# Pairwise outer products with batch normalisation: the statistics regrouped, with TensorE sums, one shift per input and another load order

## The chip, the cores and the metric

The kernel runs on one core of a Trainium2 chip. A core has five engines that run their own instruction streams side by side: TensorE (PE, matrix products), VectorE (DVE), ScalarE (ACT), GpSimd (POOL) and SyncE (SP, which here only starts DMA transfers). They meet by semaphores. Inputs and output lie in HBM; the engines work on SBUF (128 partitions), and TensorE writes to PSUM. The metric is the device time of one execution in microseconds (us). The kernel before takes 1874.52 us, the median of 7 runs (1874.37 to 1874.97).

## What is computed

The reference, cut to what matters:

```python
B, F0, F1, E, C = (256, 39, 39, 16, 1)          # the inputs themselves hold 1024 samples
_ROWS, _COLS = np.tril_indices(F1, k=-1)         # the 741 pairs row > col
cross  = xj[:, rows, :, None] * xi[:, cols, None, :]
mean   = jnp.mean(cross, axis=(0, 2, 3), keepdims=True)
var    = jnp.mean(jnp.square(cross - mean), axis=(0, 2, 3), keepdims=True)
normed = (cross - mean) * jax.lax.rsqrt(var + BN_EPS)
normed = normed * gamma[None, :, None, None] + beta[None, :, None, None]
out    = normed[:, :, None, :, :] * W[None, None, :, :, :]
```

xi and xj are 1024 x 39 x 16 in f32. For each sample and each of 741 pairs of fields a 16 x 16 outer product is formed, normalised with one mean and one variance per pair (over all samples and all 256 elements), scaled by gamma and beta of the pair and multiplied element by element by the 16 x 16 matrix W. The output is 1024 x 741 x 256 f32, 777 MB; the inputs are 6 MB.

## The kernel before

**Layout.** Sample 8p + t lies in partition p at place t, so a partition holds eight samples (NT = 8). xi_sb and xj_sb hold the inputs whole. The output is made in tiles: one row r of the triangle (r pairs) for two places t (T = 2). y_sb has room for four tiles of the middle row (r = 19) at first; the scratch tiles of the statistics lie in the parts of y_sb that later tiles take (`scratch`, parts "dev" and "rest").

**Statistics.** The mean of an outer product over its 256 elements is the product of two sums, and the mean square the product of two sums of squares. So the statistics of all pairs come from three Gram matrices over the samples, of 38 rows and 77 columns (`gram`, three accumulators ps_g; the right-hand side fb has for each place t 38 means of xi, 38 second moments and a constant). To keep precision, the data are shifted first: `sums` adds up the 16 elements of each field (VectorE), a matrix of ones on TensorE sums those of place 0 over all partitions, and this gives one shift per field and input. `deviation` subtracts the shift (GpSimd, eight steps of two places), `square` squares in place (ScalarE), `moments` adds up 16 squares (VectorE), `means` corrects the sums by the shift, `gram` multiplies. The `steps` tuple gives the order of the eight steps.

**From the Gram matrices to the scale.** A chain of small 38 x 38 steps on ScalarE, GpSimd and VectorE forms mean and variance of each pair, the reciprocal (VectorE), a square root (ScalarE, rstd) and one refinement step (VectorE) to stq, which holds scale and offset. `spread` sends row r of stq to all partitions by a matmul with the selecting matrix pick (row r of it has ones where the partition is r - 1; GpSimd makes it by one affine_select), and `apply` joins it with gamma and beta in st_sb. This goes by row groups, the group of row 19 first.

**The first tiles.** So that stores can start as soon as the scale is known, the raw outer products of tile 0 are made before: 32 products of 304 elements, one for each (t, i), by `raw_products`: steps 0 to 23 on ScalarE (raw0), 24 to 31 on GpSimd (raw0_pool), given out in small lots by `emit` between other work. After the scale is known, `affine` applies scale and offset to tile 0 in place (pairs 0 and 1 on VectorE, the others in turn on ScalarE and GpSimd), `weigh` multiplies by W on VectorE in six pieces and stores each. From tile 1 on, `scale_xi` scales xi (GpSimd), `products` makes outer products (ScalarE, and some on GpSimd), `finish` adds the offset and multiplies by W (VectorE, a few pairs on GpSimd) and stores.

**Order.** The whole is under a manual schedule: every engine executes its instructions in the order in which the code emits them, and waits at the head of its queue. DMA starts are instructions of the queue of the engine that starts them (SP and ACT here). There are eight semaphores for DMAs, so each DMA start also waits for the landing of the one eight before it.

Of the kernel before, what the change touches and what calls it, by code (L numbers as in the profile page):

```python
# [9 lines left out]
ALU = mybir.AluOpType  # L10
# [4 lines left out]
T = 2  # L15
# [11 lines left out]

LOADS = (1, 2, 3, 4, 6, 8)
# [15 lines left out]
def tile_pair_outer_batchnorm(  # L44
# [58 lines left out]
    place = {"dev": half * EE, "rest": (half + half // 2) * EE}  # L103
    stop = {"dev": (half + half // 2) * EE, "rest": 2 * half * EE}
# [18 lines left out]
    devs = [scratch("dev", P, T, G, E) for _ in range(7)]  # L123
    ones = scratch("rest", P, P)
    pick = scratch("rest", G, G, P)
    total = scratch("rest", P, NT, 2 * G)
    fa = scratch("rest", P, NT, 2 * G)
    fb = scratch("rest", P, NT, 2 * G + 1)
    shift = scratch("rest", P, 2, G)
    shift_r = scratch("rest", G, 1)  # L130
    g1 = scratch("rest", G, 2 * G + 1)
    u_u, u_2 = (scratch("rest", G, 1) for _ in range(2))
    k, q1, q2, q3, uv, uv_2, v_half, mixed, low, mean, rstd, inv = (scratch("rest", G, G) for _ in range(12))
# [13 lines left out]
    def product(n, engine, t, i, src):  # L147

        r, t0, _ = tiles[n]
        y = view(n).rearrange("p t n (i j) -> p t n i j", j=E)[:, t, :, i, :]  # L150
        scale = xj_sb[:, t0 + t, r, i : i + 1]
        if engine is nc.scalar:
            nc.scalar.activation(y, src, AF.Copy, scale=scale)  # L153
        else:
            engine.tensor_scalar(y, src, scale, 1.0, ALU.mult, ALU.mult)  # L155
# [167 lines left out]
    with tc.manual_schedule():  # L323
        nc.gpsimd.memset(ones, 1.0)
        nc.sync.dma_start(xi_sb[:, 0, 0 : F // 2], xi_v[:, 0, 0 : F // 2])
        nc.scalar.dma_start(xi_sb[:, 0, F // 2 : F], xi_v[:, 0, F // 2 : F])
        nc.sync.dma_start(xj_sb[:, 0], xj_v[:, 0])
        def load(engine, to, source, t0, t1):
            engine.dma_start(to[:, t0:t1], source[:, t0:t1])

        for t0, t1 in zip(LOADS, LOADS[1:-2]):
            load(nc.sync, xj_sb, xj_v, t0, t1)
            load(nc.scalar, xi_sb, xi_v, t0, t1)


        nc.scalar.activation(shift_r, ones[0:G, 0:1], AF.Sqrt)
        load(nc.sync, xj_sb, xj_v, *LOADS[-3:-1])
        nc.gpsimd.memset(fb[:, :, 2 * G : 2 * G + 1], 1.0 / NB)

        nc.gpsimd.affine_select(  # L340
            out=pick, in_=ones[0:G, :].unsqueeze(1).to_broadcast([G, G, P]),
            compare_op=ALU.is_equal, fill=0.0, base=0,
            pattern=[[-1, G], [0, P]], channel_multiplier=1,
        )
# [5 lines left out]
        k_s = 1.0 / (P * E)  # L350
        sources = (xj_sb[:, :, 1:F], xi_sb[:, :, 0:G])

        def part(x):
            return slice(x * G, (x + 1) * G)

        def sums(t0, t1, xs=(1, 0)):
            for x in xs:
                nc.vector.tensor_reduce(  # L358
                    total[:, t0:t1, part(x)], sources[x][:, t0:t1], AX.X, ALU.add
                )  # L360

        steps = ((0, 1), (0, 0), (2, 1), (4, 1), (6, 1), (2, 0), (4, 0), (6, 0))

        def deviation(n):
            t0, x = steps[n]
            nc.gpsimd.tensor_tensor(  # L368
                devs[n % 7],
                sources[x][:, t0 : t0 + T],  # L370
                shift[:, x : x + 1, :].unsqueeze(3).to_broadcast([P, T, G, E]),
                ALU.subtract,
            )

        def square(n):

            _, x = steps[n]
            scale = 0.25 / NB**0.5 if x else 0.25
            nc.scalar.activation(devs[n % 7], devs[n % 7], AF.Square, scale=scale)  # L379

        def moments(n, t0, t1):
            first_t, x = steps[n]
            to = fb if x else fa
            nc.vector.tensor_reduce(  # L384
                to[:, t0:t1, G : 2 * G], devs[n % 7][:, t0 - first_t : t1 - first_t], AX.X, ALU.add
            )

        def means(t0, t1):
            for x, to in enumerate((fa, fb)):
                stt(  # L390
                    to[:, t0:t1, 0:G],
                    total[:, t0:t1, part(x)],
                    1.0 / (E * NB) if x else 1.0 / E,
                    ps_u[:, x : x + 1, :].to_broadcast([P, t1 - t0, G]),
                    ALU.mult,
                    ALU.subtract,
                )

        def gram(n, t0, t1):
            x = steps[n][1]  # L400
            for t in range(t0, t1):
                terms = ((0, fa[:, t, 0:G]), (2, ones[:, 0:G])) if x else ((1, fa[:, t, G : 2 * G]),)
                for acc, lhs in terms:
                    nc.tensor.matmul(  # L404
                        ps_g[acc][0:G, 0 : 2 * G + 1], lhs, fb[:, t], start=t == 0, stop=t == NT - 1
                    )

        raw0 = raw_products(0, nc.scalar, range(24))
        raw0_pool = raw_products(0, nc.gpsimd, range(24, 32))
        ps_shift = (ps_g[0][:, 0:G], ps_s[:, 0:G])  # L410
        for x in (1, 0):
            sums(0, 1, (x,))
            nc.tensor.matmul(ps_shift[x], ones, total[:, 0, part(x)], start=True, stop=True)
        nc.tensor.matmul(ps_c[0:G, 0:1], total[:, 0, 0:G], ones[:, 0:1], start=True, stop=True)

# [179 lines left out]
```

## Time and profile before

The profiled execution took 1874.54 us; its span from the first to the last instruction is 1872.8 us.

| view | figure | value |
|---|---|---|
| times | median of 7 runs | 1874.52 us |
| profiled execution | time / span | 1874.54 / 1872.8 us |
| busy share of the span | DVE / ACT / POOL / PE | 92% / 85% / 83% / 1% |
| DMA | bytes, mean rate | 783.61 MB, 418 GB/s |
| chain that ended last | DMA of the output | 57% |
| timeline | first store issued | 34.10 us |
| GpSimd's deviations (L368) | 8 instructions of 1216 elements | 2265 ns mean |
| ScalarE's squares (L379) | 8 of 1216 elements | 1211 ns mean |
| VectorE's sums of 1216 elements (L358, L384) | | 1412 ns mean |
| raw products of 304 elements (L153 / L155) | ScalarE / GpSimd | 538 / 518 ns mean |
| Gram matmuls (L404) | 48 records, 77 columns | 337 ns mean |

The engines' shares are means over the whole span. A line such as "L153" is a line of the kernel and may be a helper that serves many stages, so the stage before the first store is read from stretches of the timeline. Instructions on an engine overlap a little: the mean duration of one is longer than the distance from one start to the next.

### The profile page before, as it was taken

What the parts mean: (1) busy time and instruction counts of PE and PEld (TensorE: products, weight loads), DVE (VectorE), ACT (ScalarE), POOL (GpSimd) and SP (SyncE); (2) the same over time, 40 slices, a digit from 0 to 9 for tenths busy, and PEclk for the clock granted to TensorE, in tenths of its full rate; (3) what the DMA queues carried; (4) which work ended last, traced back from release to release, by engine and by line L of the source; (5) the groups of instructions that cost most, each with busy time, mean ns of one, the idle gap of its engine ahead of it and who ended that gap; (6) DMA issues with size and microseconds to landing.
All of it is one profiled execution on the core that took longest, in us unless ns stands there. A gap on an engine that the chain in (4) does not pass through costs nothing.

```text
span 1872.8 us, 9236 instructions
## 1 busy us (share of the span) xinstructions
PE 26.0 (1%) x130; PEld 23.2 (1%) x130; DVE 1723.1 (92%) x2641; ACT 1584.4 (85%) x3152; POOL 1554.2 (83%) x1650
## 2 busy tenths in 40 slices
PE   5000000000000000000000000000000000000000
PEld 4000000000000000000000000000000000000000
DVE  8999888899999999999999999999999999999994
ACT  8999888898888867666799999999899998989892
POOL 9999877787777788999988888888888888888882
DMA  5999999999999999999999999999999999999998
GB/s 214 390 419 424 426 430 422 425 426 427 425 427 425 427 426 424 429 425 421 417 435 425 426 432 426 425 431 426 426 431 426 430 426 430 427 429 425 429 427 355
DMA packets 54711, 783.61 MB, mean 418 GB/s; under 512 B 4720, under 2 KB 6384, under 8 KB 17520
## 3 DMA queue, kind: packets, MB, share of 16 engines
q1 hardware_dynamic: 53344, 779.72, 98.2%
q10 hardware_dynamic: 1296, 3.29, 0.5%
q14 instruction: 70, 0.57, 0.1%
q8 instruction: 1, 0.02, 0.0%
HBM read 6.00 MB, written 776.99 MB: 418 GB/s over the span
## 4 chain that ended last, share of the span: by engine, by line
DMA 57%; ACT 20%; DVE 16%; POOL 2%; issue 1%; SPq 0%; ACTq 0%; DVEq 0%; POOLq 0%
DMA out_dram<-y_sb 57%; ACT y_sb L153 20%; DVE y_sb L313 16%; POOL y_sb L155 1%; POOL y_sb L302 1%; ACT y_sb L250 0%; POOL y_sb L299 0%; POOL xs L175 0%; SPq L236 0%; ACT y_sb L297 0%; DVE y_sb L198 0%; DVE xs L188 0%; ACTq L153 0%; DVEq L590 0%; DVE st_sb L540 0%
## 5 line engine op out<-in xcount | busy, mean ns | idle before, releaser
L313 DVE SCALAR_TENSOR_TENSOR y_sb<-y_sb,st_sb,w_dve 128x512 f32<-128x512 f32 (+1 forms) x2511 | 1653.1, 739 | 114.5 <-issue 99.1
L153 ACT ACTIVATE y_sb<-xs,xj_sb 128x144 f32<-128x144 f32 (+23 forms) x2930 | 1453.3, 586 | 239.3 <-DMA out_dram<-y_sb 204.3
L302 POOL TENSOR_TENSOR y_sb<-y_sb,w_sb 128x2048 f32<-128x2048 f32 (+3 forms) x155 | 517.8, 3347 | 89.8 <-ACT y_sb L297 80.2
L155 POOL TENSOR_SCALAR y_sb<-xs,xj_sb 128x320 f32<-128x320 f32 (+19 forms) x1006 | 559.8, 581 | 9.1 <-DMA out_dram<-y_sb 8.8
L175 POOL TENSOR_TENSOR xs<-xi_sb,st_sb 128x640 f32<-128x640 f32 (+33 forms) x135 | 184.2, 1364 | 177.5 <-ACT y_sb L153 172.8
L299 POOL TENSOR_SCALAR y_sb<-y_sb,st_sb 128x512 f32<-128x512 f32 x291 | 197.6, 695 | 5.1 <-ACT y_sb L153 5.1
L297 ACT ACTIVATE y_sb<-y_sb,st_sb 128x512 f32<-128x512 f32 x160 | 100.2, 708 | 4.0 <-POOL y_sb L155 2.3
L208 POOL TENSOR_TENSOR y_sb<-xs,xj_sb 128x1280 f32<-128x1280 f32 (+2 forms) x24 | 66.7, 2799 | 0.0
L198 DVE TENSOR_TENSOR y_sb<-xs,ps 128x256 f32<-128x256 f32 (+3 forms) x32 | 24.8, 817 | 0.6
L522 PE MATMUL ps<-y_sb 38*128 38x38 f32 (+37 forms) x76 | 16.4, 397 | 2.9 <-DVE y_sb L508 2.9
L522 PEld LDWEIGHTS ps<-y_sb 38*128 38x128 f32 x76 | 16.3, 329 | 3.2 <-DVE y_sb L508 3.2
L379 ACT ACTIVATE y_sb<-y_sb 128x1216 f32<-128x1216 f32 x8 | 9.7, 1211 | 2.9 <-POOL y_sb L368 2.6
L153 ACT ACTIVATE y_sb<-xi_sb,xj_sb 128x304 f32<-128x304 f32 x24 | 11.4, 538 | 0.0
L384 DVE TENSOR_REDUCE y_sb<-y_sb 128x76 f32<-128x1216 f32 (+1 forms) x9 | 10.9, 1271 | 0.0
L259 DVE TENSOR_TENSOR y_sb<-y_sb,w_dve 128x2048 f32<-128x2048 f32 (+4 forms) x6 | 10.7, 1839 | 0.1
L368 POOL TENSOR_TENSOR y_sb<-xi_sb,y_sb 128x1216 f32<-128x1216 f32 x4 | 9.1, 2265 | 1.2 <-DMA xi_sb<-in_r_xi_dram 1.0
L358 DVE TENSOR_REDUCE y_sb<-xi_sb 128x38 f32<-128x608 f32 (+1 forms) x6 | 5.9, 990 | 3.8 <-DMA xi_sb<-in_r_xi_dram 3.8
L368 POOL TENSOR_TENSOR y_sb<-xj_sb,y_sb 128x1216 f32<-128x1216 f32 x4 | 9.0, 2266 | 0.0
L404 PE MATMUL ps<-y_sb 128*38 128x77 f32 x48 | 8.1, 337 | 13.3 <-DVE y_sb L384 13.2
L252 POOL TENSOR_SCALAR y_sb<-y_sb,st_sb 128x512 f32<-128x512 f32 x8 | 6.4, 815 | 1.9 <-ACT y_sb L153 1.9
L358 DVE TENSOR_REDUCE y_sb<-xj_sb 128x38 f32<-128x608 f32 (+1 forms) x6 | 6.0, 992 | 0.8 <-DMA xj_sb<-in_r_xj_dram 0.7
L250 ACT ACTIVATE y_sb<-y_sb,st_sb 128x512 f32<-128x512 f32 x9 | 6.5, 801 | 0.2 <-ACT y_sb L153 0.2
(60 smaller groups left out, 42.9 us busy)
## 6 DMA issues: line engine op xcount, KB each, us to landing
out_dram<-y_sb SPq DMA_DIRECT2D x16, 3072.0 KB, 21.7
out_dram<-y_sb SPq DMA_DIRECT2D x20, 2432.0 KB, 12.5
out_dram<-y_sb SPq DMA_DIRECT2D x10, 4608.0 KB, 15.1
out_dram<-y_sb SPq DMA_DIRECT2D x12, 3840.0 KB, 21.0
out_dram<-y_sb SPq DMA_DIRECT2D x16, 2816.0 KB, 22.3
out_dram<-y_sb SPq DMA_DIRECT2D x12, 3584.0 KB, 23.1
out_dram<-y_sb SPq DMA_DIRECT2D x12, 3328.0 KB, 24.3
out_dram<-y_sb SPq DMA_DIRECT2D x15, 2560.0 KB, 11.9
```

Source lines behind the costliest of these rows:

```text
L153: nc.scalar.activation(y, src, AF.Copy, scale=scale)
L155: engine.tensor_scalar(y, src, scale, 1.0, ALU.mult, ALU.mult)
L175: nc.gpsimd.tensor_tensor(xs, xi_sb[:, t0 : t0 + T, 0:r, :], s_sb[:, :, n0 : n0 + r, :].to_broadcast([P, T, r, E]), ALU.mult,)
L198: nc.vector.tensor_tensor(view(n)[:, t].rearrange("p n (i j) -> p n i j", j=E), xs[:, t].unsqueeze(2).to_broadcast([P, r, E, E]), xj_short ...
L208: nc.gpsimd.tensor_tensor(view(n)[:, t].rearrange("p n (i j) -> p n i j", j=E), xs[:, t].unsqueeze(2).to_broadcast([P, r, E, E]), xj_sb[:, ...
L297: nc.scalar.activation(y[:, :, c, :], y[:, :, c, :], AF.Identity, bias=t_c)
L299: nc.gpsimd.tensor_scalar(y[:, :, c, :], y[:, :, c, :], t_c, 1.0, ALU.add, ALU.mult)
L302: nc.gpsimd.tensor_tensor(y[:, :, c0:c1, :], y[:, :, c0:c1, :], w_sb.unsqueeze(1).to_broadcast([P, T, c1 - c0, EE]), ALU.mult,)
L313: stt(y[:, t : t + size, c, :], y[:, t : t + size, c, :], t_sb[:, n0 + c : n0 + c + 1], w_dve.to_broadcast([P, size, EE]), ALU.add, ALU.mult,)
L358: nc.vector.tensor_reduce(total[:, t0:t1, part(x)], sources[x][:, t0:t1], AX.X, ALU.add)
L368: nc.gpsimd.tensor_tensor(devs[n % 7], sources[x][:, t0 : t0 + T], shift[:, x : x + 1, :].unsqueeze(3).to_broadcast([P, T, G, E]), ALU.sub ...
L522: nc.tensor.matmul(ps[:, :, first[r] - n0 : first[r] - n0 + r], pick[:, r - 1, :], stq[:, :, 0:r], start=True, stop=True,)
```

## The change

The statistics are rewritten between the first load and stq; the tiles behind keep their code.

- One shift per input instead of one per field: `offset` multiplies the first 19 fields of place 0 by ones on TensorE (304 columns), and an activation with an accumulator sums the columns. The shift goes into the square's bias, so `deviation` and `means` are gone, and the correction of the sums moves into small 38 x 1 constants.
- The sums of the elements of four places of each input (xi: places 2 to 5, xj: 0 to 3) are made on TensorE: 16 matmuls with a unit matrix, one for each element, summed in PSUM (`matrix_sums`). The other places stay with VectorE (`sums`).
- Four of the squared blocks are halved by GpSimd (`fold`: element e plus element e + 8) before VectorE sums them.
- Loads: all of xi first, one place at a time, then xj, then gamma, beta and W. All but two are started by SP. Row 19 of xj for places 0 and 1 comes early, as a small load of its own (xj_first), and the raw products of tile 0 read it there.
- Raw products of tile 0: 20 on GpSimd (12 of them at the start), 12 on ScalarE (2 ahead of the square root, 10 behind it). The copy of W into PSUM (w_dve) follows them.
- pick is made in two parts: rows 18 to 38 at the start, rows 1 to 17 behind the affines of tile 0.

```diff
+        load(nc.scalar, xi_sb, xi_v, 2, 3)
+        nc.sync.dma_start(xj_first, xj_v[:, 0:T, mid])
+        load(nc.sync, xi_sb, xi_v, 1, 2)
+        for t in range(3, NT):
+            load(nc.sync, xi_sb, xi_v, t, t + 1)
+        for t0, t1 in ((0, 1), (1, 2), (2, 4), (4, 6), (6, 7), (7, 8)):
             load(nc.sync, xj_sb, xj_v, t0, t1)
-            load(nc.scalar, xi_sb, xi_v, t0, t1)
+        nc.sync.dma_start(st_sb[:, 0], gamma.partition_broadcast(P))
+        nc.sync.dma_start(st_sb[:, 1], beta.partition_broadcast(P))
+        nc.sync.dma_start(w_sb[:, 0, :], w.rearrange("o i j -> (o i j)").partition_broadcast(P))
...
+        picks(mid - 1, F)
...
+        def offset(x):
+            start = xi_sb[:, 0, 0:mid] if x else xj_sb[:, 0, 1 : mid + 1]
+            nc.tensor.matmul((ps_c, ps_s)[x][:, 0 : mid * E], ones, start.rearrange("p f e -> p (f e)"), ...)
+            nc.scalar.activation(junk, (ps_c, ps_s)[x][:, 0 : mid * E], AF.Copy,
+                scale=-scale_q[x] / (P * mid * E), accum_out=bias_q[:, x : x + 1])
+        def square(x, t0, t1):
+            nc.scalar.activation(of_squares(x, t0, t1), sources[x][:, t0:t1], AF.Square,
+                bias=bias_q[:, x : x + 1], scale=scale_q[x])
+        def fold(to, of):
+            nc.gpsimd.tensor_tensor(to, of[..., 0:H], of[..., H:E], ALU.add)
+        def shifted(t0, t1, of):
+            nc.scalar.activation(fb[:, t0:t1, 0:G], of, AF.Identity, bias=bias_m, scale=1.0 / (E * NB))
+        def matrix_sums(x, t0, t1):
+            ps = ps_half[x][:, 0 : (t1 - t0) * G].rearrange("p (t f) -> p t f", f=G)
+            for e in range(E):
+                nc.tensor.matmul(ps, unit, sources[x][:, t0:t1, :, e], start=e == 0, stop=e == E - 1)
+            return ps
-        raw0 = raw_products(0, nc.scalar, range(24))
-        raw0_pool = raw_products(0, nc.gpsimd, range(24, 32))
+        raw0 = raw_products(0, nc.scalar, (*range(12, 16), *range(24, 32)))
+        raw0_pool = raw_products(0, nc.gpsimd, (*range(12), *range(16, 24)))
+        offset(1)
+        emit(raw0_pool, 12)
+        sums(1, 0, 1); sums(1, 1, 2)
+        square(1, 0, 2); seconds(1, 0, 2); square(1, 2, 4); seconds(1, 2, 4)
+        times(bias_m, bias_q[:, 1:2], 4.0 / NB**0.5)
+        shifted(0, 2, total[:, 0:2])
+        square(1, 4, 6)
+        ps_xi = matrix_sums(1, 2, 6)
+        seconds(1, 4, 6); sums(1, 6, 8)
+        square(1, 6, 8); fold_squares(1, 6, 8); seconds(1, 6, 8, H)
+        offset(0)
+        square(0, 0, 2)
+        shifted(2, 6, ps_xi); shifted(6, 8, total[:, 6:8])
+        square(0, 2, 4); fold_squares(0, 0, 2)
+        ps_xj = matrix_sums(0, 0, 4)
+        gram(2, 0, 8)
...
+        square(0, 4, 6); sums(0, 4, 6); seconds(0, 0, 2, H); fold_squares(0, 2, 4)
+        gram(1, 0, 2)
+        square(0, 6, 7); square(0, 7, 8)
+        nc.scalar.copy(fa[:, 0:4, 0:G], ps_xj)
+        gram(0, 0, 6)
+        sums(0, 6, 7); seconds(0, 2, 4, H); gram(1, 2, 4)
+        sums(0, 7, 8); gram(0, 6, 8)
+        fold_squares(0, 4, 6); seconds(0, 4, 6, H); gram(1, 4, 6)
+        for t in (6, 7):
+            seconds(0, t, t + 1); gram(1, t, t + 1)
...
+        nc.gpsimd.tensor_tensor(q1, q1, q4, ALU.add)
+        emit(raw0_pool, 32)
...
+        nc.vector.reciprocal(inv, p_var)
+        emit(raw0, 2)
         nc.scalar.activation(rstd, inv, AF.Sqrt)
         emit(raw0, 32)
+        nc.scalar.copy(w_dve, w_sb)
...
         affine(0, range(12, mid))
+        picks(1, mid - 1)
         weigh(0)
```

Several statements of the new code are drawn together on one line here. `seconds` is the new name of `moments`; `times` is a ScalarE copy with a scale.

## The prediction

> **What bounds the kernel now.** I read the busy time by stretches first, since the page's shares are means over two unlike stages.
>
> ```profile
> 20.00:34.00 14.00, 7.50 (x41) 5.91 (x41) 11.71 (x25) 13.29 (x28) 11.75 (x21) 1.00 0.01 4
> 34.00:60.00 26.00, 13.79 (x65) 13.65 (x64) 25.86 (x46) 26.00 (x56) 25.32 (x37) 1.00 0.91 359
> 60.00:70.00 10.00, 0.00 (x0) 0.00 (x0) 9.97 (x18) 10.00 (x24) 9.14 (x13) 1.00 0.76 307
> 100.00:1800.00 1700.00, 0.00 (x0) 0.00 (x0) 1586.92 (x2426) 1461.24 (x2882) 1427.83 (x1496) 1.00 1.00 426
> ```
>
> The last columns are the DMA's share and its GB/s. From 100 us on the DMA is at 1.00: the output leaves at 426 GB/s and no engine matters. From 20 to 34 us it is at 0.01: the loads are in, nothing can be stored. So the end is the first store's time, plus the bytes, plus what the DMA loses until about 70 us, where the engines barely keep ahead. The change edits the work before the first store, and one piece (a GpSimd select) behind it. The timeline, engine by engine, of that stage:
>
> ```profile
> 12.83 0.96 PE L404 MATMUL ps<-y_sb 128*38 128x77 f32 x6 [5.78 <-DVE y_sb L384]
> 27.96 0.47 PE L404 MATMUL ps<-y_sb 128*38 128x77 f32 x2 [0.22 <-DVE y_sb L384]
> 31.36 16.42 PE L522 MATMUL ps<-y_sb 38*128 38x38 f32 x76 [2.92 <-DVE y_sb L508]
> ...
> 28.34 1.86 ACT L153 ACTIVATE y_sb<-xi_sb,xj_sb 128x304 f32<-128x304 f32 x4
> 30.23 2.29 ACT L153 ACTIVATE y_sb<-xi_sb,xj_sb 128x304 f32<-128x304 f32 x5
> 32.66 0.56 DVE L252 TENSOR_SCALAR y_sb<-y_sb,st_sb 128x512 f32<-128x512 f32 x1
> 33.26 0.69 DVE L259 TENSOR_TENSOR y_sb<-y_sb,w_dve 128x512 f32<-128x512 f32 x1
> 34.10 27.71 SPq L236 DMA_DIRECT2D out_dram<-y_sb  x15
> ...
> 1.08 4.51 POOL L340 TENSOR_SCALAR_AFFINE_SELECT y_sb<-y_sb 38x4864 f32<-38x4864 f32 x1
> 18.00 6.71 POOL L368 TENSOR_TENSOR y_sb<-xj_sb,y_sb 128x1216 f32<-128x1216 f32 x3
> ```
>
> The last Gram product ends at 28.43 (27.96 + 0.47). From there to the first affine (DVE, 32.66) is a tail of 4.23 us, and its last stretch is ScalarE's raw products, which end at 32.52: the affine rewrites in place what every raw product wrote, so it waits for all 32. I call the first affine's start F; F is 32.66 now, and everything behind it keeps its order.
>
> **What goes.** GpSimd's eight deviations (18.1 us by the page's two L368 groups, the last three in the line above), twelve of ScalarE's 24 raw products (12 x 0.46 = 5.5 us, from four in 1.86), the shift copies and the mean corrections. GpSimd gets twelve raw products at 0.50 (four took 2.01) from about 4.5 to 10.5 us and four folds at 1.22 (the 608-element L175 row); it has room. VectorE's work shrinks. None of this sets the end, because a new engine comes onto the path.
>
> **What comes: TensorE.** Two sets of 16 matmuls of 152 columns against the unit matrix, two of 304 columns, and the same 24 Gram matmuls. An f32 matmul is two records (24 Gram matmuls stand as 48). Six Gram records in 0.96 us, the last lasting 0.335 (their median), start (0.96 - 0.335)/5 = 0.125 us apart, 1.62 ns a column. The 76 records of L522 with 128-wide weights and at most 76 columns start 16.42/76 = 0.216 apart, for few columns as for many: there the weights set the pace. The new matmuls have both 128-wide weights and 152 columns. Bounds: 0.125 (columns cost nothing more), 0.216 (weights alone), 0.247 (152 x 1.62, the weights hidden), 0.463 (both, one after the other). I take 0.247: columns outlast weights here, and L522 shows the weight load hidden. Thus 32 x 0.247 = 7.9 us a set, and 2 x 304 x 1.62 = 1.0 us for a 304-column one.
>
> TensorE is in order, and the set for xi stands ahead of xj's offset matmul, on which every square of xj on ScalarE waits (through the accumulation). Its account:
> - xi of samples 2 to 5 landed: the first load lands at 3.8 (VectorE idles until 3.84), each further 312 KB takes 0.77 us at about 415 GB/s (slices from 5 to 10 us: 396 to 418), five more make 7.7; the xj slice in 64-byte runs ahead of them costs between 0 and 0.8, I take 0.4: 8.1.
> - set for xi 7.9: 16.0. Offset of xj 1.0: 17.0. Set for xj (landed by about 12.5): 24.9.
> - 24 Gram matmuls x 0.25 = 6.0: 30.9, and 0.2 until the last result: 31.1, against 28.43 now.
>
> ScalarE does not bound this: it idles from 11 to 17.5, then needs an accumulation 0.55, three squares of 1.1, two of 0.6, three shifts 0.55, eleven small ones 1.4: 7.0, ending near 24.3, where it waits for the xj set.
>
> **The tail.** Gram matrix 0 is complete four matmuls (1.0 us) before the last. Then two dependent ScalarE steps (0.5) and four dependent GpSimd steps at 0.33 (26.66, 26.98, ... in the 38x38 rows): 1.85 - 1.0 = 0.85 after the end. VectorE's three 38x38 steps (0.22 each) and the reciprocal 0.39: 1.05, with hand-overs 1.1. The square root follows within 0.2. Behind it ScalarE still has ten raw products, 10 x 0.46 + 0.1 = 4.7, while VectorE, TensorE and the three st_sb steps need only about 2.3. Tail: 0.85 + 1.1 + 0.2 + 4.7 = 6.85 against 4.23, so F = 31.1 + 6.85 = 37.95: 5.3 later. The w_dve copy (0.37) now stands behind the raw products; VectorE's own affine (0.56) hides it, else 0.3.
>
> **Moved past F.** The rows below 18 of the select, 2176 of 4864 elements: 4.51 x 2176/4864 = 2.0 us on GpSimd between its affines and tile 1's products, in the stretch where it is 25.32 of 26 us busy. It now waits 0.52 there for ScalarE (before L175), and tile 2's products end at 58.03 where VectorE takes them up at 58.63: 0.6 of slack. 2.0 - 0.5 - 0.6 = 0.9; bounds 0.3 and 2.0; I take 1.0, straight into the DMA gaps of 60 to 70 us. The matmuls behind the select wait some 7 us more, and their results are wanted only from 69 us on.
>
> **Moved DMAs.** SP issues 17 loads (6 now) at 0.43 each, ACT two. gamma, beta and w land near 17 to 18 us instead of 19 to 21, long before their use; the first store's issue waits on none. Nothing.
>
> Sum: 5.3 + 1.0 = 6.3 on the profiled execution's own 1874.54 (span 1872.8, 1.7 around it), which is the median's 1874.52 too: **1880.8 us**. With 0.216 instead of 0.247 the sets lose 2.0 us together: 1878.8.
>
> **Two rules weighed.** In the L522 row the pace stays 0.216 over 16.4 us; nothing in this trace shows TensorE speeding up. The Trainium skill (TensorE: Matmul & The Clock Gate, Part 1) says that the array idles at half its clock and that some 3.4 us of sustained activity release it; by that the second half of the first set and everything after would run at double pace, F would be near 32.5, and the time about 1875.5, an estimate. Against the change speaks the skill's SBUF page (SBUF — State Buffer, Door 1: The DMA port swizzle): an f32 read that steps over more than four elements crosses a 16-byte line each time and is penalised, and the new matmuls step by sixteen; no run here shows such a read, and no price stands there.
>
> **Rivals.**
> 1. TensorE's records cost 0.125 (not slower). For it: a stretch as dense as the new sets does not exist in the trace, so L522's pace may be the weights' alone. Then the xi set takes 4.0 and its offset 0.5: ScalarE restarts at 12.9, works 7.0, and with 0.9 of waits and the copy fa is whole by 20.8, 14 Gram matmuls (3.5) end at 24.3, F = 31.15: 1.5 earlier. With the select's 1.0 that is 1874.0. It decides from about 0.17 a record down (F 33, within 0.2%).
> 2. The stepping reads are slower: at 0.3 the sets grow by 3.4 us, 1884.2; at 0.463 by 13.8, 1894.6. The trace has no row for or against it.
> 3. Faster by more than 3.75 us: needs rival 1, loads in by 7.5 (0.6), the select's 2.0 hidden, and small ScalarE steps at half: 1874.5 - 1.5 - 0.6 - 1.6 = 1870.8 at best. Little speaks for it: the ten raw products behind the square root stay, 4.7 us.
> That the products don't reach TensorE is excluded by the program's order: 16 matmuls of 152 columns stand there twice.
>
> **How the numbers follow.** A run tells about 0.2% (3.75 us) from no change. Forecast, records of 0.21 to 0.25: 0.45 (1878.5 to 1882). Rival 1 and the middle, 0.125 to 0.2: 0.41 (1873 to 1878). Rival 2: 0.08. Rival 3: 0.06. Slower 0.45 + 0.08 = 0.53, same 0.41, faster 0.06. The range 1873 to 1883 leaves out rival 3, most of rival 2 and a little of rival 1, 0.2 together.
>
> **What would show it.** In the new trace: 16 matmuls of 152 columns lasting 7.9 us from about 8.1; ScalarE idle before the second accumulation until about 17; a last Gram product near 31; F near 38; ten raw products between the square root and F; GpSimd's late select of 2.0 us and VectorE waiting for L155 near 64. Sets of 4 us or a first store before 34 would make the forecast wrong.

## The result, and the profile after

The changed kernel takes 1879.59 us, the median of 15 runs (1879.16 to 1880.35), against 1874.54 us for the kernel before (35 runs beside them, 1874.31 to 1874.97). The ratio is 1.0027, with a 95% interval of 1.002 to 1.0034, which leaves out no change: slower by 5.05 us. The profiled execution took 1879.45 us with a span of 1877.7.

First the same stretches as before. The columns after the length are busy time (and instructions) of PE, PEld, DVE, ACT and POOL, then the granted clock of TensorE, the share of the DMA and its GB/s:

```profile
20.00:34.00 14.00, 10.00 (x79) 8.35 (x77) 7.19 (x17) 10.57 (x34) 8.56 (x15) 1.00 0.01 2
34.00:60.00 26.00, 15.18 (x72) 14.83 (x71) 23.05 (x40) 24.36 (x52) 23.84 (x32) 0.50 0.69 270
60.00:70.00 10.00, 0.00 (x0) 0.00 (x0) 9.31 (x18) 10.00 (x24) 9.83 (x13) 0.50 1.00 398
100.00:1800.00 1700.00, 0.00 (x0) 0.00 (x0) 1588.41 (x2429) 1461.87 (x2885) 1430.03 (x1495) 0.50 1.00 426
```

From 100 us on nothing has changed: 426 GB/s, the DMA full. The loss lies ahead. From 20 to 34 us VectorE, ScalarE and GpSimd all do less than before (7.19 against 11.71 us on VectorE), and TensorE does more. From 34 to 60 us the DMA's share is 0.69 in the place of 0.91: stores start later. The time in which no transfer runs at all, added up from the DMA records, is 24.8 us against 19.5. That difference of 5.3 accounts for the loss (4.91 between these two executions).

The timeline of the stage (start, length, engine, line, operation, shapes, count, and in brackets the idle time before and what ended it):

```profile
8.59 8.61 PE L427 MATMUL ps<-xi_sb,y_sb 128*128 128x152 f32 x32 [3.28 <-DMA xi_sb<-in_r_xi_dram]
17.02 0.69 PE L375 MATMUL ps<-xj_sb,y_sb 128*128 128x304 f32 x2
17.55 8.43 PE L427 MATMUL ps<-xj_sb,y_sb 128*128 128x152 f32 x32
17.75 0.42 ACT L382 ACTIVATE y_sb<-ps 128x304 f32<-128x304 f32 x1 [6.17 <-PE ps L375]
25.91 3.42 PE L435 MATMUL ps<-y_sb 128*38 128x77 f32 x48
28.83 0.35 ACT L510 ACTIVATE y_sb<-ps,y_sb 38x1 f32<-38x1 f32 x1 [1.15 <-PE ps L435]
30.83 0.19 DVE L529 SCALAR_TENSOR_TENSOR y_sb<-ps,y_sb 38x38 f32<-38x38 f32 x1 [2.78 <-POOL y_sb L520]
32.05 0.24 ACT L535 ACTIVATE y_sb<-y_sb 38x38 f32<-38x38 f32 x1 [0.95 <-DVE y_sb L533]
32.19 4.48 ACT L157 ACTIVATE y_sb<-xi_sb,y_sb 128x304 f32<-128x304 f32 x10
36.76 0.55 DVE L256 TENSOR_SCALAR y_sb<-y_sb,st_sb 128x512 f32<-128x512 f32 x1 [2.53 <-ACT y_sb L157]
38.18 25.25 SPq L240 DMA_DIRECT2D out_dram<-y_sb  x14
44.46 2.12 POOL L354 TENSOR_SCALAR_AFFINE_SELECT y_sb<-y_sb 38x2176 f32<-38x2176 f32 x1
63.69 2.72 DVE L317 SCALAR_TENSOR_TENSOR y_sb<-y_sb,st_sb,w_dve 128x512 f32<-128x512 f32 x4 [0.69 <-POOL y_sb L159]
```

Read the four PE lines first: 8.59, 17.02, 17.55, 25.91, each without an idle bracket after the first, up to the last Gram product at 25.91 + 3.42 = 29.33. TensorE is the path for 20.7 us on end. ScalarE stands idle for 6.17 us until the offset matmul behind the first set lets it go on. Then the tail: square root at 32.05, ten raw products until 36.67, and VectorE idle for 2.53 until they are done. F is 36.76 (32.66 before) and the first store 38.18 (34.10 before). Tile 2, the last line above, starts 26.93 us behind F; in the kernel before it starts at 58.56, 25.90 behind F. VectorE waits for GpSimd, behind whose late select the products queue up. 4.10 + 1.03 = 5.13, against 5.05 measured.

### The profile page after: what moved, and what is told of

The parts are those of the page before. It is cut to its first block, busy times and chain, and to the rows that moved or that the text cites. A ratio compares the mean times of both kernels' runs of the same rounds, so it can differ in the third digit from the quotient of the medians.

```text
span 1877.7 us, 9371 instructions
## 1 busy us (share of the span) xinstructions
PE 37.9 (2%) x192; PEld 33.8 (2%) x192; DVE 1714.3 (91%) x2627; ACT 1582.4 (84%) x3154; POOL 1547.9 (82%) x1657
## 3 DMA queue, kind: packets, MB, share of 16 engines
HBM read 6.02 MB, written 776.99 MB: 417 GB/s over the span
## 4 chain that ended last, share of the span: by engine, by line
DMA 54%; ACT 20%; DVE 16%; POOL 4%; issue 2%; SPq 0%; ACTq 0%; DVEq 0%; POOLq 0%
DMA out_dram<-y_sb 54%; ACT y_sb L157 20%; DVE y_sb L317 16%; POOL y_sb L159 2%; POOL xs L179 1%; POOL y_sb L303 1%; POOL y_sb L306 0%; POOL y_sb L256 0%; SPq L240 0%; POOL y_sb L354 0%; ACTq L157 0%; DVE xs L192 0%; DVEq L624 0%; DVE st_sb L573 0%; DVE ps L566 0%
## 5 line engine op out<-in xcount | busy, mean ns | idle before, releaser
L317 DVE SCALAR_TENSOR_TENSOR y_sb<-y_sb,st_sb,w_dve 128x512 f32<-128x512 f32 (+1 forms) x2511 | 1653.2, 739 | 115.0 <-issue 96.2
L301 ACT ACTIVATE y_sb<-y_sb,st_sb 128x512 f32<-128x512 f32 x160 | 100.2, 708 | 3.9 <-POOL y_sb L159 2.3
L202 DVE TENSOR_TENSOR y_sb<-xs,ps 128x256 f32<-128x256 f32 (+3 forms) x32 | 24.8, 817 | 0.5
L555 PE MATMUL ps<-y_sb 38*128 38x38 f32 (+37 forms) x76 | 15.8, 384 | 14.5 <-POOL y_sb L354 10.5
L555 PEld LDWEIGHTS ps<-y_sb 38*128 38x128 f32 x76 | 15.5, 314 | 14.8 <-POOL y_sb L354 10.7
L410 DVE TENSOR_REDUCE y_sb<-y_sb 128x76 f32<-128x608 f32 (+2 forms) x9 | 8.7, 994 | 7.5 <-POOL y_sb L403 6.7
L403 POOL TENSOR_TENSOR y_sb<-y_sb 128x608 f32<-128x608 f32 x4 | 5.9, 1474 | 9.3 <-ACT y_sb L391 9.3
L159 POOL TENSOR_SCALAR y_sb<-xi_sb,y_sb 128x304 f32<-128x304 f32 x20 | 10.0, 519 | 0.8 <-DMA y_sb<-in_r_xj_dram 0.8
L427 PE MATMUL ps<-xi_sb,y_sb 128*128 128x152 f32 x32 | 8.6, 441 | 3.3 <-DMA xi_sb<-in_r_xi_dram 3.3
L427 PE MATMUL ps<-xj_sb,y_sb 128*128 128x152 f32 x32 | 8.4, 435 | 0.0
L427 PEld LDWEIGHTS ps<-xi_sb,y_sb 128*128 128x128 f32 x32 | 7.6, 271 | 4.7 <-issue 4.1
L427 PEld LDWEIGHTS ps<-xj_sb,y_sb 128*128 128x128 f32 x32 | 6.6, 205 | 1.7
## 6 DMA issues: line engine op xcount, KB each, us to landing
out_dram<-y_sb SPq DMA_DIRECT2D x12, 3328.0 KB, 24.3
```

The costliest lines, as they stand in the source:

```text
L202: nc.vector.tensor_tensor(view(n)[:, t].rearrange("p n (i j) -> p n i j", j=E), xs[:, t].unsqueeze(2).to_broadcast([P, r, E, E]), xj_short ...
L301: nc.scalar.activation(y[:, :, c, :], y[:, :, c, :], AF.Identity, bias=t_c)
L317: stt(y[:, t : t + size, c, :], y[:, t : t + size, c, :], t_sb[:, n0 + c : n0 + c + 1], w_dve.to_broadcast([P, size, EE]), ALU.add, ALU.mult,)
L410: nc.vector.tensor_reduce(to, of, AX.X, ALU.add)
L427: nc.tensor.matmul(ps, unit, sources[x][:, t0:t1, :, e], start=e == 0, stop=e == E - 1)
L555: nc.tensor.matmul(ps[:, :, first[r] - n0 : first[r] - n0 + r], pick[:, r - 1, :], stq[:, :, 0:r], start=True, stop=True,)
```

## Experiments

Each kernel is the changed one with one edit, unless said otherwise. "Before" is the kernel before, run beside it on the same chip: median 1874.44 for the first four kernels, 1874.26 for the one that keeps the stepping read beside matmuls on constants and for the last two, 1874.21 for the other four. A "record" is one entry of the trace for a matmul; an f32 matmul has two.

### What holds the TensorE sets: adjacent columns

Sixteen matmuls of 152 columns as before, but each reads 152 adjacent columns of the flat input in the place of every 16th. It adds up other elements than the sums need.

```diff
-                    ps, unit, sources[x][:, t0:t1, :, e], start=e == 0, stop=e == E - 1
+                    ps_half[x][:, 0:n], unit, flat_x[:, at : at + n], start=e == 0, stop=e == E - 1
```

> The unit-matrix matmuls read 152 adjacent columns in place of every sixteenth one; the sums are then of the wrong elements, the work is the same in number and size. Theory (the stepping read sets the pace, 0.26 us a record at either clock): the second set runs at about 0.13 a record, 4.1 us instead of 8.4; the first gains only after the clock is released near 13.6 us, 6.5 to 7 us instead of 8.6; the last Gram product ends near 26.5 instead of 29.3, the first affine starts near 34 instead of 36.8, the time is 1876 to 1877. Rival (the two loads of 128-wide weights set the pace): both sets stay at 8.4 to 8.6 us and the time at 1879.6. A rival in between: 0.216 a record as in the selecting matmuls, 6.9 us a set, 1878.

Measured: 1873.67 (1871.99 to 1875.15, 10 runs), ratio 0.9993 (0.9984 to 1.0002). The TensorE lines of its timeline:

```profile
4.95 6.75 PE L430 MATMUL ps<-xi_sb,y_sb 128*128 128x152 f32 x32
11.53 0.67 PE L375 MATMUL ps<-xj_sb,y_sb 128*128 128x304 f32 x2
12.04 4.30 PE L430 MATMUL ps<-xj_sb,y_sb 128*128 128x152 f32 x32
```

The second set takes 16.27 - 12.04 = 4.23 us, 0.132 a record, where the changed kernel needs 0.261. Its records start 0.253 apart until 9.89, where the trace's record of the granted clock goes to 1.00, and 0.129 apart from there. So neither the 128-wide weights nor the 152 columns cost more than 0.129 at full clock; the stepping read does. The time came out below what was expected, for a reason that was overlooked: a matmul of adjacent columns reads one place, or two neighbouring ones, in the place of all four, so the set began at 4.95, right behind the first offset matmul, and not at 8.59. Pace and start are mixed in this time; the runs of four below keep the sums whole. The ten runs of this kernel lie 3.16 us apart, more than those of any other kernel here; why is not shown.

### How far a read may step

Each set made of four matmuls of each step 1, 2, 4 and 8, the columns as many as before. Other elements are added here too; there is one execution.

```diff
+            for k in range(4):
+                nc.tensor.matmul(ps_half[x][:, 0:n], unit, stepped(4, k), start=False, stop=False)
...
```

> In each set of 16 unit-matrix matmuls four read every column, four every second, four every fourth, four every eighth (wrong sums, same sizes), each step on a line of its own. Theory of the stepping read with a line of four elements: at full clock steps 1 and 2 (perhaps 4) at about 0.13 us a record, step 8 at about 0.26. If the pace falls with the number of elements per line, step 2 lies between. Rival (weights): all four alike at 0.21 to 0.26. At half clock all four alike at about 0.25 by both.

Measured: 1873.46. Steps 1, 2, 4 and 8 in this order, first the set for xi, then the one for xj:

```profile
5.00 2.15 PE L435 MATMUL ps<-xi_sb,y_sb 128*128 128x152 f32 x8
6.98 1.23 PE L437 MATMUL ps<-xi_sb,y_sb 128*128 128x152 f32 x8
8.05 2.32 PE L439 MATMUL ps<-xi_sb,y_sb 128*128 128x152 f32 x8
...
12.93 1.20 PE L435 MATMUL ps<-xj_sb,y_sb 128*128 128x152 f32 x8
13.96 1.24 PE L437 MATMUL ps<-xj_sb,y_sb 128*128 128x152 f32 x8
15.04 2.32 PE L439 MATMUL ps<-xj_sb,y_sb 128*128 128x152 f32 x8
17.18 2.38 PE L441 MATMUL ps<-xj_sb,y_sb 128*128 128x152 f32 x8
```

The first line is at half clock (the clock goes up at 6.93): 1.98 us from start to start for eight records. At full clock steps 1 and 2 take 1.03 and 1.08, step 4 takes 2.14, step 8 2.31. The price comes at once between two and four f32 (16 bytes) and changes little behind it: 0.268 and 0.289 a record, and step 16 is at 0.261 in the changed kernel. At half clock the stepping read costs next to nothing: 0.258 a record with it (changed kernel, before 13.77), 0.253 without.

### The late select

```diff
-        picks(mid - 1, F)
+        picks(1, F)
...
-        picks(1, mid - 1)
```

> The whole select at the start again, nothing of it behind the affines. Theory (the late select holds tile 1's and tile 2's GpSimd products up and so VectorE): VectorE starts tile 2 about 26.0 us behind the first affine, as before the change, instead of 26.9; the time falls by 0.9 us to 1878.7. Rival (the DMA's gaps after the first store swallow it): no change, 1879.6.

Measured: 1878.73 (1878.14 to 1879.77, 10 runs), ratio 1.0023 (1.0014 to 1.0033), 0.76 less above the kernel before than the changed kernel is. The intervals of the two ratios overlap, so the time alone doesn't show the gain; the trace shows the wait gone. VectorE goes from tile 1 to tile 2 without one:

```profile
38.17 0.55 DVE L256 TENSOR_SCALAR y_sb<-y_sb,st_sb 128x512 f32<-128x512 f32 x1 [2.29 <-ACT y_sb L157]
50.73 15.37 DVE L317 SCALAR_TENSOR_TENSOR y_sb<-y_sb,st_sb,w_dve 128x256 f32<-128x256 f32 x37
```

The changed kernel has two brackets in L317 there (0.18 and 0.69); here there is none, and tile 2 starts 25.88 us behind F in the place of 26.93. F is late here, 38.17, because in this execution xi's place 1 landed at 7.42 in the place of 6.02 and everything behind moved with it; it is the slowest of the kernel's ten runs (1879.77). Why a load lands late in one execution stays open.

### The raw products behind the square root

```diff
+        emit(raw0, 10)
         offset(0)
         square(0, 0, 2)
```

> Ten of ScalarE's twelve raw products moved into its idle time ahead of the second accumulation. Theory (the ten raw products behind the square root set the first affine): the affine then waits for the three st_sb steps, 34.4 us instead of 36.8, and the time falls by 2.3 us to 1877.3. Rival (something else holds the affine or the first store, or the DMA loses the gain again by 75 us): less than 0.5 us.

Measured: 1877.50 (1877.12 to 1877.73, 11 runs), ratio 1.0015 (1.0006 to 1.0024). ScalarE's ten raw products run in its idle time, and F is 35.00:

```profile
11.68 4.49 ACT L157 ACTIVATE y_sb<-xi_sb,y_sb 128x304 f32<-128x304 f32 x10
...
30.98 3.98 POOL L159 TENSOR_SCALAR y_sb<-xi_sb,y_sb 128x304 f32<-128x304 f32 x8
35.00 0.55 DVE L256 TENSOR_SCALAR y_sb<-y_sb,st_sb 128x512 f32<-128x512 f32 x1 [0.33 <-POOL y_sb L159]
```

F now comes 0.33 us after VectorE is ready, and what it waits for is GpSimd: its last eight raw products are next in line. The time is 1.99 us nearer to the kernel before than the changed kernel is.

### The sums on VectorE

```diff
-        ps_xi = matrix_sums(1, 2, 6)
+        sums(1, 2, 4); sums(1, 4, 6)
-        ps_xj = matrix_sums(0, 0, 4)
-        nc.scalar.copy(fa[:, 0:4, 0:G], ps_xj)
+        sums(0, 0, 2); sums(0, 2, 4)
```

> The changed kernel with the element sums of all samples on VectorE (four reductions of two samples, 1.41 us each, in the place of the two TensorE sets and of the copy out of PSUM). Theory (TensorE's sets set the end, through the offset matmul queued behind the first and the Gram products behind the second): the offset matmul of xj goes at 11 in the place of 17.02, ScalarE's idle 6.17 before the second accumulation shrinks under 1, the last Gram product ends near 25 (VectorE has 19 us of reductions from 4.0 on) in the place of 29.33, F near 32.4, the time 1879.6 - 4.4 = 1875.2 (1874.5 to 1876.5). Rival (the order of the loads, xi before xj, is what costs, whoever adds): xj lands at 16.4 as before, ScalarE's squares of xj and VectorE's reductions behind it end no earlier than 27, F above 35, the time over 1877.8.

Measured: 1874.36 (1873.86 to 1875.62, 11 runs), ratio 1.0001 (0.9992 to 1.001). The second offset matmul goes when its data are in, and ScalarE's idle 6.17 is 0.92:

```profile
11.24 1.38 PE L375 MATMUL ps<-xj_sb,y_sb 128*128 128x304 f32 x2 [5.98 <-DMA xj_sb<-in_r_xj_dram]
12.66 0.42 ACT L382 ACTIVATE y_sb<-ps 128x304 f32<-128x304 f32 x1 [0.92 <-PE ps L375]
20.75 4.49 PE L435 MATMUL ps<-y_sb 128*38 128x77 f32 x32 [3.88 <-DVE y_sb L410]
...
32.00 0.55 DVE L256 TENSOR_SCALAR y_sb<-y_sb,st_sb 128x512 f32<-128x512 f32 x1 [2.29 <-ACT y_sb L157]
```

The last Gram product ends at 25.24 and F is 32.00. Taking the sets off TensorE gives back 4.9 us (5.05 over the kernel before falls to 0.15), with the late select and the long tail still in. The new order of loads, the rival, does not hold the end. The time is just under the range expected.

### Runs of four on TensorE

The same sums on TensorE, reading four neighbouring elements at a time; four partial sums for each field go to PSUM and VectorE adds them.

```diff
-            for e in range(E):
-                nc.tensor.matmul(ps, unit, sources[x][:, t0:t1, :, e], start=e == 0, stop=e == E - 1)
+            for t, bank in zip(range(t0, t1, T), ...):
+                for e in range(0, E, 4):
+                    nc.tensor.matmul(ps, unit, sources[x][:, t : t + T, :, e : e + 4], ...)
...
+            reduce((total if x else fa[:, :, 0:G])[:, t : t + T], ps)
```

> The changed kernel with TensorE reading runs of four neighbouring elements (16 bytes) in the place of one element of every 16: four matmuls of 304 columns for two samples, 2432 columns a set as before, whose four partial sums VectorE adds (128x304 to 76). It begins when samples 2 and 3 are in, near 6.9. Theory (a read is paid for each 16 bytes touched, not for each jump): a set of 2432 columns in two records each takes 4.1 us at full clock and about 8 at half, the clock is released about 5 us after the first set's start, so the first set lasts 6.5 to 7 and ends by 14, the second 4.1; ScalarE restarts at 14.5 in the place of 17.75, the last Gram product ends near 25, F near 32.4, the time 1875.2 (1874.5 to 1876.5). Rival (a jump costs whatever it carries): 38 jumps by 4 columns in the place of 152 single ones give a pace between, or the same 8.4 us a set, and the time stays at 1878 to 1880.

Measured: 1874.01 (1873.59 to 1874.82, 11 runs), ratio 0.9998 (0.999 to 1.0007). TensorE:

```profile
7.00 6.52 PE L432 MATMUL ps<-xi_sb,y_sb 128*128 128x304 f32 x16 [1.84 <-DMA xi_sb<-in_r_xi_dram]
13.36 0.68 PE L375 MATMUL ps<-xj_sb,y_sb 128*128 128x304 f32 x2
13.87 4.26 PE L432 MATMUL ps<-xj_sb,y_sb 128*128 128x304 f32 x16
...
24.45 0.33 PE L445 MATMUL ps<-y_sb 128*38 128x77 f32 x2 [0.37 <-DVE y_sb L410]
...
31.11 0.55 DVE L256 TENSOR_SCALAR y_sb<-y_sb,st_sb 128x512 f32<-128x512 f32 x1 [2.29 <-ACT y_sb L157]
```

The second set takes 4.26 us for the 2432 columns that took 8.43: what counts is how many f32 are read of each 16 bytes, not that the read jumps. The last Gram product ends at 24.78, as expected, and F is 31.11, 1.3 earlier than expected, which puts the time just under its range: the tail is 6.33 us in the place of 7.43, since the last Gram products wait for VectorE while ScalarE's steps on Gram matrix 0 (from 22.30) are done ahead of them.

### With TensorE kept busy from the start

To the runs of four, 15 matmuls of 128 columns on constants are added around the first offset matmul; their results are not used.

```diff
+        warm(7)
         offset(1)
+        warm(8)
```

> The kernel with runs of four, and 15 matmuls of 128 columns on constants ahead of and behind the first offset matmul (1 to 8 us, results unused), so that TensorE is busy before the first set. Theory (the clock counts now that the read is no longer the limit): the clock is released near 6 to 7, the first set takes 4.1 to 4.5 us in the place of 6.5 to 7, the second offset matmul waits for its data only (11), ScalarE restarts near 12, the last Gram product ends near 22 to 23, F near 30, the time 1872 to 1873.5. Rival (by then loads and ScalarE bind): less than 1 us under the kernel with runs of four alone. Second rival: the matmuls ahead delay the first offset and with it ScalarE and the raw products; then no gain.

Measured: 1872.90 (1872.48 to 1873.59, 11 runs), ratio 0.9992 (0.9984 to 1.0001), 1.11 under the runs of four alone. The clock's record goes up at 7.05:

```profile
7.87 4.29 PE L432 MATMUL ps<-xi_sb,y_sb 128*128 128x304 f32 x16
...
24.12 0.47 PE L449 MATMUL ps<-y_sb 128*38 128x77 f32 x2 [0.37 <-DVE y_sb L410]
```

The first set falls from 6.52 to 4.29, as expected; the last Gram product ends at 24.59, not at 22 to 23, since it now waits for VectorE, and VectorE for GpSimd's last fold behind ScalarE's squares. So both the theory (for the set) and the first rival (for the end) hold in part; the gain of 1.11 lies just above that rival's bound of 1. This profiled execution, the slowest of the 11, had its loads some 0.7 us later.

### The same matmuls on constants, with the stepping read kept

```diff
+        warm(7)
         offset(1)
+        warm(8)
```

> The changed kernel, its reads of every 16th element kept, with 15 matmuls of 128 columns on constants ahead of and behind the first offset matmul, as in the kernel with runs of four. Theory (the read of every 16th element is the limit, at either clock): the clock is released before the first set, and its records stay at 0.258; the last Gram product ends near 29, the time 1879.6 (1878.9 to 1880.3). Rival (the half clock is what holds the first set, and the second is slow for another reason): the first set takes 4.1 to 5 us, ScalarE restarts 3 to 4 us earlier, the time near 1876.

Measured: 1879.09 (1878.62 to 1879.63, 8 runs), ratio 1.0026 (1.0016 to 1.0036). The clock's record goes up at 6.62, before the first set:

```profile
9.29 8.50 PE L427 MATMUL ps<-xi_sb,y_sb 128*128 128x152 f32 x32 [1.47 <-DMA xi_sb<-in_r_xi_dram]
17.61 0.69 PE L375 MATMUL ps<-xj_sb,y_sb 128*128 128x304 f32 x2
18.14 8.43 PE L427 MATMUL ps<-xj_sb,y_sb 128*128 128x152 f32 x32
```

8.50 us wholly at full clock, for 8.61 where the clock came up in the middle, as the theory said. The clock is worth nothing to the sets as long as the read is the limit.

### VectorE's sums with the other two costs removed

To the kernel with sums on VectorE: whole select at the start, ten of ScalarE's raw products behind its last square, GpSimd's last eight between the folds.

```diff
-        picks(mid - 1, F)
+        picks(1, F)
...
         fold_squares(1, 6, 8)
+        emit(raw0_pool, 3)
...
         square(0, 7, 8)
+        emit(raw0, 10)
```

> Element sums on VectorE, the whole select at the start, ten of ScalarE's raw products before the tail in the place of behind the square root, GpSimd's last eight between the folds. Theory (the costs found are separate and add): from the run with VectorE's sums alone 1.0 less for the select and about 2.5 less for the tail (4.2 to 5 us from the last Gram product to F in the place of 7.43): F near 29.5, the time 1871 to 1872. Rival (VectorE or ScalarE is full by then, so what leaves the tail lands ahead of it): F no earlier than 31.5 and the time above 1873.5.

Measured: 1873.93 (1873.13 to 1874.62, 11 runs), ratio 0.9997 (0.9989 to 1.0006): the theory missed by 2 us, and the rival was right.

```profile
21.85 4.48 ACT L157 ACTIVATE y_sb<-xi_sb,y_sb 128x304 f32<-128x304 f32 x10
26.24 0.45 ACT L440 ACTIVATE y_sb<-ps,y_sb 38x38 f32<-38x38 f32 x2
...
32.24 0.55 DVE L256 TENSOR_SCALAR y_sb<-y_sb,st_sb 128x512 f32<-128x512 f32 x1
```

In the kernel with VectorE's sums alone ScalarE took up Gram matrix 0 at 24.09; here it takes up the chain's first step only at 26.24, behind ten raw products. The work that left the tail stood in front of it, and F is where it was (32.24 for 32.00). Four ahead and six behind is the next kernel:

```diff
-        emit(raw0, 10)
+        emit(raw0, 4)
```

> The kernel with sums on VectorE, early select and early raw products, with four of ScalarE's raw products ahead of the tail in the place of ten (two ahead of the square root, six behind it). Theory (its miss came from ScalarE: ten raw products kept it until 26.3, while Gram matrix 0 was whole at 24.1): ScalarE is free by then, the square root comes at 27.3 to 27.6 in the place of 29.78, six raw products (2.8 us) behind it just cover VectorE's and TensorE's last steps (2.46), F near 30.2, the time 1871.9 (1871.3 to 1872.6). Rival (VectorE is what is late, and the raw products lay in its shadow): the square root stays near 29.5, F at 32, the time 1873.9.

Measured: 1871.62 (1871.34 to 1872.55, 11 runs), ratio 0.9986 (0.9977 to 0.9995).

```profile
27.68 0.23 ACT L540 ACTIVATE y_sb<-y_sb 38x38 f32<-38x38 f32 x1 [0.89 <-DVE y_sb L538]
27.82 2.72 ACT L157 ACTIVATE y_sb<-xi_sb,y_sb 128x304 f32<-128x304 f32 x6
30.58 0.55 DVE L256 TENSOR_SCALAR y_sb<-y_sb,st_sb 128x512 f32<-128x512 f32 x1 [0.48 <-ACT y_sb L157]
```

The time is in the range expected. The square root comes 2.1 us earlier, and VectorE waits for the raw products only 0.48. Twelve raw products cost as much as ever; what counts is which gap they lie in.

### A version that beats both

Runs of four, matmuls on constants, the whole select early; ScalarE's eleven small steps in its two waits; raw products shared 23 to 9 between GpSimd and ScalarE and laid into the gaps.

```diff
-        raw0 = raw_products(0, nc.scalar, (*range(12, 16), *range(24, 32)))
-        raw0_pool = raw_products(0, nc.gpsimd, (*range(12), *range(16, 24)))
+        raw0 = raw_products(0, nc.scalar, (15, *range(24, 32)))
+        raw0_pool = raw_products(0, nc.gpsimd, (*range(15), *range(16, 24)))
...
         square(0, 0, 2)
+        times(u, bias_q[0:G, 0:1], -4.0)
...
         square(0, 7, 8)
+        emit(raw0, 2)
...
-        emit(raw0, 2)
+        emit(raw0, 3)
         nc.scalar.activation(rstd, inv, AF.Sqrt)
```

> Runs of four and the matmuls on constants, the whole select at the start, ScalarE's eleven small steps in its two waits ahead of the squares of xj, three more raw products for GpSimd (seven of its 23 behind the Gram chain), and nine for ScalarE (two ahead of the chain, three ahead of the square root, four behind it). Theory (what is left ahead of F are ScalarE's work behind the second accumulation and the raw products, and the costs add): the last square of xj ends near 20, the last Gram product near 22.7, the square root near 24.5, F 26.9 to 27.5, the time 1868.7 to 1869.4. Rival (VectorE, with its sums, is next): the last Gram product stays at 24, F near 28.5, the time near 1870.5. Second rival (the DMA runs dry behind an earlier start): F as told, the time above 1871.

Measured: 1869.27 (1868.97 to 1869.51, 7 runs), ratio 0.9973 (0.9963 to 0.9984): 5.0 us faster than the kernel before, and so 10.0 faster than the changed one, each held against the kernel before beside it.

```profile
23.06 0.33 PE L449 MATMUL ps<-y_sb 128*38 128x77 f32 x2 [0.37 <-DVE y_sb L410]
25.01 0.23 ACT L559 ACTIVATE y_sb<-y_sb 38x38 f32<-38x38 f32 x1
25.15 1.85 ACT L157 ACTIVATE y_sb<-xi_sb,y_sb 128x304 f32<-128x304 f32 x4
27.27 0.17 DVE L597 TENSOR_TENSOR st_sb<-ps,st_sb 128x19 f32<-128x19 f32 x1
27.57 0.56 DVE L256 TENSOR_SCALAR y_sb<-y_sb,st_sb 128x512 f32<-128x512 f32 x1
```

The tail is 27.57 - 23.39 = 4.2 us in the place of 7.43; the raw products end at 27.00, and F follows on VectorE's own last step at 27.27. The last Gram product came at 23.39 where 22.7 was expected.

### All kernels on one account

The start of tile 2 on VectorE holds both F and the late select. The account is that start less 58.56, the start in the kernel before; beside it stands the profiled time less the median of the kernel before on that chip (us). Tile 2 starts 25.9 us behind F where the whole select is early, and 26.8 to 26.9 behind it where a part is late.

| kernel | F | tile 2 starts | account | measured |
|---|---|---|---|---|
| changed | 36.76 | 63.69 | +5.13 | +4.91 |
| adjacent columns | 31.14 | 58.06 | -0.50 | -0.80 |
| steps 1 to 8 | 30.79 | 57.71 | -0.85 | -0.98 |
| select early | 38.17 | 64.05 | +5.49 | +5.33 |
| raw products early | 35.00 | 61.91 | +3.35 | +3.06 |
| sums on VectorE | 32.00 | 58.82 | +0.26 | +0.25 |
| runs of four | 31.11 | 57.95 | -0.61 | -0.51 |
| runs of four, constants | 30.92 | 57.75 | -0.81 | -0.62 |
| VectorE, all early | 32.24 | 58.19 | -0.37 | -0.15 |
| stepping, constants | 37.34 | 64.17 | +5.61 | +5.34 |
| VectorE, fitted | 30.58 | 56.46 | -2.10 | -2.16 |
| runs of four, fitted | 27.57 | 53.46 | -5.10 | -5.29 |

No row is off by more than 0.3. The whole matter of this kernel is F and the select; the 1815 us behind tile 2's start are the DMA's.

## Why the prediction was right, step by step

The size was right and the verdict too; the reason for its main term held for the first third of it only, and that the sum came out is in part luck. The terms as the prediction put them, with what the profile after has:

| term | predicted | measured | difference |
|---|---|---|---|
| start of the first set | 8.1 | 8.59 | +0.49 |
| both sets and the offset between | 16.8 | 25.91 - 8.59 = 17.32 | +0.52 |
| Gram products | 6.2 | 3.42 | -2.78 |
| tail | 6.85 | 36.76 - 29.33 = 7.43 | +0.58 |
| late select | 1.0 | 26.93 - 25.90 = 1.03 | +0.03 |
| all | +6.3 | +5.13 | -1.16 |

- **The records at 0.247.** The number held (0.263 and 0.261 a record over the two sets). It was taken as 152 columns at 1.62 ns, the pace of the Gram products before. That reason holds for the first 20 of the 64 records: up to 13.77 they start 0.258 apart, where adjacent columns at half clock start 0.253 apart. For the other 44 it fell. The trace has the clock at full from 13.77 on, and at full clock 152 adjacent columns take 0.129 to 0.132. What kept these records at 0.26 is rival 2's mechanism, the stepping read, at a price that happens to be the half clock's. The prediction weighed both causes, each by itself, the clock for faster and the read for slower; they came together and cancelled. That was luck.
- **The Gram products at 0.25.** This is the term that was mis-sized: 0.142 a matmul (3.42 / 24). They read 77 adjacent columns and so had the full gain of the clock, 2.8 us.
- **"Nothing in this trace shows TensorE speeding up."** True of that trace, and no ground for the new one, where TensorE is busy without a gap for 20 us. Of the two skill rules weighed, the release of the clock (TensorE: Matmul & The Clock Gate, Part 1) happened (at 13.77, 5.2 us into the first set), and the time of 1875.5 drawn from it did not come, because the other rule (SBUF — State Buffer, Door 1: The DMA port swizzle) decided: reads that cross a 16-byte line each time. The runs show its price, a factor of two at full clock. They put the edge lower than the prediction's "more than four elements": a step of four f32 pays in full, a step of two nothing, which agrees with that page's sentence on at least two hits per line.
- **The weights setting the pace at 0.216 in L522.** That pace is the half clock's: in the changed kernel the same row matmuls (L555) start 0.111 apart until the clock falls back at 34.25, and 0.214 apart behind it. Beside 152 columns the 128-wide weights don't show at either clock (0.253 and 0.129 with adjacent columns), so the choice of 0.247 over 0.463 was right. That the weights are what holds the row matmuls was not tested.
- **Loads.** xi's places 2 to 5 were in at 8.46, for 8.1 said. The other loads don't set the end: the first store waits for none, and with the sums on VectorE the kernel with the new order is even with the kernel before.
- **ScalarE and its idle time.** Said: idle from 11 to 17.5, done by 24.3. The trace: idle 6.17 until 17.75, its last square ends at 25.69, and it waits 0.33 for the set, so TensorE, not ScalarE, held the path.
- **The tail.** Its main part was right: 4.57 us from the start of the ten raw products to F, for 4.7. Its beginning was 1.50 long for 0.85: the chain of small steps took 2.0 (28.83 to 30.83) for 1.85, and Gram matrix 0 led the last matmul by 0.50 (28.83 to 29.33) for 1.0. A faster TensorE shortens the Gram products and also the shadow that they cast. Moving all ten products away shortens the tail by 1.96 us (7.43 to 35.00 - 29.53 = 5.47; 29.53 is the end of that run's last Gram product) and not by the 2.53 that VectorE stood idle, since GpSimd's eight, behind the same chain, come next; the prediction didn't name them.
- **The late select.** 1.03 for 1.0, mostly VectorE's two waits (0.18 and 0.69). The run without it has tile 2 at 25.88 behind F and gave 0.76 between medians. The reading behind the term was slightly off: tile 2 is taken up at 58.56 in the kernel before, not at 58.63, which leaves 0.53 of slack for 0.6.
- **Rival 1** (0.125 a record, F 31.15, 1874.0) did not come, since the read forbade it. The runs of four, whose second set has that pace, have F at 31.11 and 1874.01; that both numbers meet the rival's is partly chance, since its first set takes 6.52 and its tail 6.33.
- **Counts off the path.** SP has seven loads in the kernel before, not six. Behind the second accumulation ScalarE has two shifts and twelve small steps, not three and eleven, and its work there took 7.94 us (17.75 to 25.69) for 7.0. A fold took 1.47 us for 1.22. None of these set F.

## What to carry to other kernels

When work moves to an engine that the trace shows only lightly used, its pace there has two parts, the clock and the way operands are read; take both from rows with the same access pattern, or keep both bounds, since a right sum may rest on two errors. Where only the order of a summation is at stake, let a matmul read four neighbouring f32 (16 bytes) at a time: it halved the sets here, and only then was a released clock worth anything. Work taken out of a tail must be laid into a gap that is measured; ten raw products ahead of the chain cost as much as behind it, four ahead and six behind cost half a microsecond.

## What the hardware showed unasked

- A stepping read hides the release of the clock altogether: at half clock the read of every sixteenth f32 is all but free (0.258 a record for 0.253), at full clock it doubles the record (0.26 for 0.129).
- The granted clock changes in units: the stretches at full clock last 3.41, 10.24, 13.65, 17.07, 20.48 and 27.31 us in the twelve traces that have such records, all multiples of 3.413, which is the window that the Trainium skill states (TensorE: Matmul & The Clock Gate, Part 1). Two kernels busy in the same way from 3.8 us on had the release at 6.93 (steps 1 to 8) and at 9.89 (adjacent columns): in these two traces the windows don't begin with the work. The release came 3 us earlier in one than in the other, and with it the price of the matmuls between.
- With the clock back at half in the tail, the first 16 records of the row matmuls (`spread`) take 3.66 us (runs of four); they take 2.84 where it is full for the first 0.9 us of them (changed kernel, until 34.25). The trace of the kernel before has no clock records and shows 1.00 throughout, but its 76 row records took 16.42 us, as they do at a recorded 0.50 (16.39): a column of 1.00 without a record is no measurement.
- One load of 312 KB landed at 6.02 in one execution and at 7.42 in another with the same loads ahead of it. All that waits for xi moved with it, by 1.4 us, about as much as the runs of one kernel lie apart here (1.0 to 1.8 us in most); whether that is its cause in the runs without a trace was not measured.
